# Four images through a windowed-attention layer: side work handed out by counts and due dates

## The chip, the core and the metric

The kernel runs on one core of one Trainium2 chip. The core has five engines that run their own instruction streams and meet at semaphores: TensorE (PE in the profile; its weight loads are PEld), VectorE (DVE), ScalarE (ACT), GpSimd (POOL) and SyncE (SP), which here issues the DMA transfers. The metric is the device time of one execution in microseconds (us); a kernel's time is the median of its runs.

## The reference, cut to what matters

The program is one forward pass over 4 images of 64 x 64 tokens with 128 channels, through four layers. The change lies in the last one, layer 3. What it computes, for each image (4096 tokens):

```python
t = t + L2_ffn(...)                      # the end of layer 2: its last addition is made in layer 3's loop
# attention over overlapping windows of 144 tokens, a new one each 72 tokens (55 windows)
xb  = ln(t) @ w_down.T + b_down          # 128 -> 16 channels
q, k, v = split(xb[windows] @ in_proj_w.T + in_proj_b)     # 4 heads of 4 channels
att = softmax(q k^T / 2) v, projected, the windows added back and divided by their overlap
out = ln(t) + sigmoid(gate) * (att @ w_up.T + b_up)
t   = t + ln(out) * gamma + beta
# a mixture of 8 experts, the best 2 of them for each token
p   = softmax(ln(t) @ router_w + router_b); top 2 of p, made to sum to 1
t   = t + sum over the two of p_e * (ln(t) @ expert_w[e] + expert_b[e])
```

Everything is float32. The work on one image does not depend on another image; only the steps inside one image follow each other.

## The kernel before

Layers 0 to 2 and the weights of layer 3 take the first 8.4 ms and are not touched. `layer3` then holds four images `b` = 0 to 3, each of which passes through these pieces:

- **Blocks** (first half of `front`, L2120 on): 8 blocks of 512 tokens. For each: `combined` (4 matmuls, L2038, and an addition on DVE), `statistics` (DVE, and a power on POOL, L2007), `normalise` (4 ACT instructions, L2017), four transposes (L2024), a copy on ACT (L2140), `downward` (4 matmuls, L2049). Each block needs about 7 `yield`s, 57 in all. The result `xb` (16 channels) goes to DRAM (`xb_d`).
- **Parts** (the rest of `front`): `windows` reads `xb_d` back, laid over partitions (8 DMAs, L2063); 16 empty steps; `queries`, 5 groups of 12 steps, makes `kt`, `qm`, `vt` with matmuls (L2179, L2185, L2195) and ACT copies (L2165).
- **Local attention**: 14 window groups for an image, four quarters each. `largest` (L2224) makes scores for their maxima (DVE, L2230), `weights` (L2266) makes scores and ACT's exponentials (L2273), `values` (L2291) multiplies with v, `divided` (L2311) divides.
- **Back** (`back`, L2351 on): 16 steps of transposes (L2358), then 8 blocks of 5 steps with matmuls (L2376), the layer norm, and the addition to `t`.
- **Chosen** (`chosen`, which calls `some` twice, once for each half image, L2407 on): the experts. A half begins with about 34 steps of layer norm, router matmuls (L2429) and the choice of two experts, then come 4 blocks with 4 transposes and 4 bias matmuls (L2480, L2489) and 8 expert matmuls of 128 x 512 (L2500), each followed by four DVE instructions that add the weighted result to the token tile `tex` (L2506). Images 0 to 2 do this with `own_bank`, one PSUM bank under the name `x`; image 3 does it in `last`, with `free_bank`, two PSUM buffers under the name `s`.

These pieces are Python generators. The order on TensorE is the order in which the code emits (the loop stands under `manual_schedule` for PE); the order on the other engines is found by the scheduler of the language from what PE's order and the data ask for.

**The loop.** `T` runs over 56 window groups (14 for each image), with `largest` four groups ahead, and `x` over 4 quarters. In this text X = 4(T + 4) + x numbers the quarters: 0 to 247, and 56 X are one image's share of `largest`. Beside the attention instructions each X holds five calls of `step(light)` and four calls of `step(heavy)`; a call takes the first generator of the list one `yield` further. `light` holds the fronts and backs, `heavy` the experts. With 57 + 76 steps a front takes some 27 X; after it `light` is empty until the image's attention has ended (`merged`, at X = 76, 132, 188 and 244), where `passed(b - 1)`, which is `back` and, behind its last step, the hand-over of `chosen` to `heavy`, and then the front of image b + 1 are put into `light` together. A front that isn't done when its image's `largest` begins (X = 56, 112, 168) is run to its end there. After the loop the rest of both lists is emitted in turns.

Of the kernel before, what the change touches and what calls it, by code (L numbers as in the profile page):

```python
# [14 lines left out]
P = 128  # L15
B = 4
HW = 64
S = HW * HW
NT = S // P
D = 128  # L20
# [28 lines left out]
DK = 16  # L49
# [11 lines left out]
def tl(pool, shape, tag, dtype=F32, bufs=None):  # L61
    return pool.tile(shape, dtype, name=tag, tag=tag, bufs=bufs)
# [1780 lines left out]
NM = (NW + G3 - 1) // G3  # L1843
# [102 lines left out]
def layer3(cm, kit, xa, wt_d, oe_d, x2, out):  # L1946
# [6 lines left out]
    with ExitStack() as ctx:  # L1953
        ctx.enter_context(nc.allow_non_contiguous_dma(reason="windows laid over partitions"))
        bp = ctx.enter_context(tc.tile_pool(name="cb", bufs=1))
# [8 lines left out]
        dr = ctx.enter_context(tc.tile_pool(name="cdram", bufs=2, space=DRAM))  # L1964
# [3 lines left out]
        wq4, wk4, f, mroot = [kit[n] for n in ("wq4", "wk4", "f", "mroot")]  # L1968
# [20 lines left out]
        def rows(a, b, k):  # L1989
            return a[b, k * BLK : (k + 1) * BLK, :].rearrange("(t p) c -> p t c", p=P)  # L1990

        def block(a, b, k, tag="tin"):
            t = tl(tp, [P, 4, D], tag)
            nc.sync.dma_start(t, rows(a, b, k))
            return t

        def statistics(src, who=""):

            st = tl(p2, [P, 4, 6], "ln_st" + who)
            mv = tl(p2, [P, 4, 2], "ln_mv" + who)  # L2000
            rs = tl(p2, [P, 2, 4], "ln_rs" + who)
            for i in range(4):
                nc.vector.bn_stats(st[:, i, :], src[:, i, :])
            for i in range(4):
                nc.vector.bn_aggr(mv[:, i, :], st[:, i, :])
            nc.vector.tensor_scalar(rs[:, 0, :], mv[:, :, 1], 1e-5, None, ALU.add)  # L2006
            nc.gpsimd.tensor_tensor(  # L2007
                rs[:, 0, :], rs[:, 0, :], mroot.to_broadcast([P, 4]), ALU.pow
            )
            nc.vector.scalar_tensor_tensor(  # L2010
                rs[:, 1, :], mv[:, :, 0], -1.0, rs[:, 0, :], ALU.mult, ALU.mult
            )
            return rs

        def normalise(dst, src, rs):
            for i in range(4):
                nc.scalar.activation(  # L2017
                    dst[:, i, :], src[:, i, :], AF.Identity,
                    bias=rs[:, 1, i : i + 1], scale=rs[:, 0, i : i + 1],
                )  # L2020

        def turned4(ps, src):
            for i in range(4):
                nc.tensor.transpose(ps[:, i * P : (i + 1) * P], src[:, i, :], cm.ident)  # L2024

        img = {}

        def gates(b, k):
            half = slice((b % 2) * E2, (b % 2 + 1) * E2)
            w = tl(tp, [P, BLK], "w")  # L2030
            nc.sync.dma_start(w[half, :], wt_d[half, b // 2, k * BLK : (k + 1) * BLK])
            return w

        def combined(b, k, t, w, ps):

            half = slice((b % 2) * E2, (b % 2 + 1) * E2)
            for i in range(4):
                nc.tensor.matmul(  # L2038
                    ps[:, i * P : (i + 1) * P], lhsT=w[half, i * P : (i + 1) * P],
                    rhs=oute[half, b // 2, :], start=True, stop=True,  # L2040
                )
            flat = t.rearrange("p i c -> p (i c)")
            nc.vector.tensor_tensor(flat, flat, ps, ALU.add)
            nc.sync.dma_start(rows(x2, b, k), t)
# [13 lines left out]
        def windows(xb_d, i):  # L2058
            for par in range(2):
                nw = (min(NM, NW - i * NM) + 1 - par) // 2  # L2060
                t0 = (i * NM + par) * STRIDE
                m0 = par * NM // 2
                nc.sync.dma_start(  # L2063
                    f[32 * i : 32 * i + DK, m0 : m0 + nw, :].rearrange(
                        "c m (j d) -> c (m j) d", d=DK
                    ),
                    xb_d[t0 : t0 + nw * WIN, :].rearrange("(m c) d -> c m d", c=DK),
                )

        def fresh(b):  # L2070
            img[b] = {"xl": tl(dr, [1, S, D], "xl_d"), "t": tl(dr, [1, S, D], "t_d")}
            return img[b], tl(bp, [P, NT, DK], "xb"), tl(dr, [S, DK], "xb_d")

        def first(b):

# [44 lines left out]
        def front(b, bank):  # L2120

            me, xb, xb_d = fresh(b)
            t, w = block(xa, b, 0), gates(b, 0)
            yield
            for k in range(NBLK):
                combined(b, k, t, w, bank())
                yield
                if k + 1 < NBLK:
                    nt, nw = block(xa, b, k + 1), gates(b, k + 1)
                rs = statistics(t)  # L2130
                yield
                yield
                xl = tl(tp, [P, 4, D], "xl")
                normalise(xl, t, rs)
                nc.sync.dma_start(rows(me["xl"], 0, k), xl)
                yield
                ps = bank()
                turned4(ps, xl)
                xT = tl(p2, [P, BLK], "xT")
                nc.scalar.copy(xT, ps)  # L2140
                yield
                yield
                downward(bank(), xT, xb, k)
                t, w = nt, nw
                yield
            nc.sync.dma_start(xb_d.rearrange("(t p) d -> p t d", p=P), xb)

            for i in range(G):
                windows(xb_d, i)
            for _ in range(16):
                yield
            yield from queries(b, bank, (nc.scalar.copy,))
# [244 lines left out]
        def chosen(b, bank):  # L2401

            me = img[b]
            for half in range(2):
                yield from some(me["t"], b, NB * half, bank)
# [110 lines left out]
        AHEAD = 4  # L2516
        LAST = B * NM
        light, heavy = [], []

        def step(todo):  # L2520
            while todo:
                try:
                    next(todo[0])
                    return
                except StopIteration:
                    todo.pop(0)

        def passed(b, bank):

            yield from back(b, bank)  # L2530
            if b + 1 < B:
                heavy.append(chosen(b, own_bank))

        def last():

            for half in range(2):
                while img[B - 1].get("done", 0) < NB * (half + 1):
                    yield
                yield from some(img[B - 1]["t"], B - 1, NB * half, free_bank)


        with tc.manual_schedule(engines={mybir.EngineType.PE}):
            first(0)
            fronts = {1: front(1, shared_bank)}
            light.append(fronts[1])
            for T in range(-AHEAD, LAST + 2):
                b, m = divmod(T + AHEAD, NM)
                if m == 0 and 0 < b < B:
                    while fronts[b] in light:
                        step(light)  # L2550
                for x in range(4):
                    if 0 < T <= LAST:
                        values(T - 1, x)
                    step(heavy)
                    step(light)
                    if x % 2 == 0 and T + AHEAD < LAST:
                        largest(T + AHEAD, x // 2)
                    step(light)
                    if x == 2 and T % 2 == 0 and 1 < T + AHEAD <= LAST:
                        turned(T + AHEAD - 1)  # L2560
                    step(heavy)
                    step(light)
                    if x == 2 and 0 < T <= LAST:
                        divided(T - 1, 0)
                    if x == 0 and 1 < T:
                        divided(T - 2, 1)
                        b, m = divmod(T - 1, NM)
                        if m == 0:
                            merged(b - 1)
                            light.append(passed(b - 1, shared_bank))  # L2570
                            if b + 1 < B:
                                fronts[b + 1] = front(b + 1, shared_bank)
                                light.append(fronts[b + 1])
                    step(heavy)
                    step(light)
                    if 0 <= T < LAST:
                        weights(T, x // 2, x % 2)
                    step(heavy)
                    step(light)
            heavy.append(last())  # L2580
            while light or heavy:
                step(light)
                step(heavy)


# [98 lines left out]
```

## Time and profile before

| | us |
|---|---|
| median of 3 runs (10190.57 to 10219.28) | 10200.37 |
| the profiled execution | 10193.03 |
| its span, first to last instruction | 10191.1 |
| layer 3's loop and tail within the span | 8424.6 to 10191.1 |

The whole program keeps PE busy for 85% of the span, DVE for 74%, ACT for 52% and POOL for 53%; the mean granted TensorE clock is 0.907 of full speed. Layer 3 is the last 1766 us, 17% of the span, and there PE is busy most.

The stages of layer 3 can be found in the trace by the `weights` matmuls of L2266: 1792 are recorded, eight for each of the 224 X from 16 to 239. The first group starts at 8539.2 us (X = 16), and counting on gives each X a time: X = 26 at 8590.6, 56 at 8684.4, 76 at 8750.6, 88 at 8826.4, 112 at 9035.3, 132 at 9148.0, 144 at 9251.9, 168 at 9451.4, 188 at 9574.0, 200 at 9675.2 and 239 at 9872.6.

### The profile page before, as it was taken

Reading aid. Unit: us, or ns where it says so; the run is one execution under the profiler, and the core shown is the slowest. Engines: PE = TensorE matmul, PEld = TensorE weight load, DVE = VectorE, ACT = ScalarE, POOL = GpSimd, SP = SyncE. Lnnn points to the kernel's source line nnn. Section 1 sums busy time; section 2 is a strip of 40 time slices with the busy share of each in tenths; the row PEclk is TensorE's granted clock in tenths of the full one; section 3 lists DMA queues with packets and bytes.
Section 4 is the critical chain, followed back from the end, with each engine's and each line's share of the span. In section 5 each row is a group of like instructions: output and inputs, shape, how many; then the busy total and the mean of one; then the engine's idle time right before and its main releaser. Section 6 shows DMA issues by size and latency. Waiting matters only on the chain.

```text
span 10191.1 us, 193260 instructions
## 1 busy us (share of the span) xinstructions
PE 8632.5 (85%) x73048; PEld 4244.2 (42%) x73048; DVE 7500.6 (74%) x11046; ACT 5339.3 (52%) x13284; POOL 5376.2 (53%) x2789
## 2 busy tenths in 40 slices
PE   7888988889988898888788659999999857888876
PEld 3333444444434444444333434444444434544442
DVE  4999999999999999999999666354541123455556
ACT  5775545665556665466422237676776513433331
POOL 4999999899999899998999300000000000100000
PEclk8999999999999999999998779999999977797887
DMA  7344543445543455444323311111100161213101
GB/s 209 104 133 128 141 132 115 124 132 144 151 115 122 122 155 146 127 121 119 95 88 93 113 52 36 37 36 37 32 24 27 45 202 36 56 27 69 42 24 47
DMA packets 1081627, 957.38 MB, mean 94 GB/s; under 512 B 165356, under 2 KB 825616, under 8 KB 1073920
## 3 DMA queue, kind: packets, MB, share of 16 engines
q1 hardware_dynamic: 1055298, 880.82, 29.3%
q0 software_dynamic: 18560, 63.37, 3.3%
q8 instruction: 586, 9.60, 0.4%
q14 instruction: 337, 2.76, 0.1%
q10 hardware_dynamic: 6846, 0.83, 0.1%
HBM read 608.77 MB, written 335.80 MB: 93 GB/s over the span
## 4 chain that ended last, share of the span: by engine, by line
PE 42%; DVE 27%; POOL 9%; issue 8%; ACT 6%; DMA 5%; SPq 2%; DVEq 0%; ACTq 0%; POOLq 0%
DVE big L869 15%; POOL big L884 8%; PE qk L1653 7%; PE av L1712 7%; PE yp L904 5%; PE db L849 5%; DVE tex L2506 2%; PE x L2500 2%; PE s L2266 2%; DVE du L825 2%; DVE mx L2230 1%; PE po L2291 1%; PE bg L383 1%; DMA xo<-xT_d 1%; DVE db L864 1%
## 5 line engine op out<-in xcount | busy, mean ns | idle before, releaser
L884 POOL TENSOR_TENSOR big<-big,ct 128x2048 f32<-128x2048 f32 x1024 | 4659.3, 4550 | 76.2 <-PE db L849 0.2
L869 DVE TENSOR_TENSOR_SCAN big<-dA,db 128x1024 f32<-128x1024 f32 x2048 | 4570.9, 2273 | 11.8 <-DMA xo<-xT_d 8.8
L849 PE MATMUL db<-dg,du 32*64 32x256 f32 x32768 | 1908.6, 417 | 639.9 <-DVE big L869 500.4
L904 PE MATMUL yp<-big,both 128*64 128x256 f32 x16384 | 2206.8, 416 | 63.1 <-ACT yc L918 50.9
L904 PEld LDWEIGHTS yp<-big,both 128*64 128x64 f32 x16384 | 1184.9, 148 | 1022.5 <-issue 547.7
L849 PEld LDWEIGHTS db<-dg,du 32*64 32x64 f32 x32768 | 655.4, 134 | 1838.3 <-issue 1737.2
L1712 PE MATMUL av<-e,x 128*128 128x512 f32 x2048 | 974.0, 592 | 4.6 <-ACT e L1707 4.6
L1653 PE MATMUL qk<-a,xT 128*128 128x512 f32 x2048 | 966.6, 594 | 8.6 <-ACT e L1657 7.9
L1657 ACT ACTIVATE e<-qk,nk 128x512 f32<-128x512 f32 x1024 | 692.8, 685 | 533.8 <-PE qk L1653 532.7
L918 ACT COPY yr<-yp 128x64 f32<-128x64 f32 x1024 | 221.4, 216 | 1417.7 <-PE yp L904 1402.0
L817 ACT ACTIVATE dg<-mask,BT 128x32 f32<-128x32 f32 x4096 | 896.6, 318 | 11.0 <-PE db L849 8.8
L772 ACT ACTIVATE dA<-dp,A 128x252 f32<-128x252 f32 x2048 | 866.1, 498 | 62.2 <-issue 42.6
L1232 POOL TENSOR_TENSOR g_rs<-g_rs,qrow 128x4 f32<-128x4 f32 x32 | 41.1, 1283 | 1500.0 <-DVE g_rs L1231 1500.0
L1653 PEld LDWEIGHTS qk<-a,xT 128*128 128x128 f32 x2048 | 378.0, 190 | 462.3 <-issue 357.7
L1712 PEld LDWEIGHTS av<-e,x 128*128 128x128 f32 x2048 | 381.6, 190 | 434.8 <-issue 393.7
L1707 ACT ACTIVATE e<-e 128x1024 f32<-128x1024 f32 x510 | 538.7, 1056 | 15.4
L876 POOL TENSOR_TENSOR cy<-big,a 128x32 f32<-128x32 f32 x1008 | 364.1, 361 | 317.5 <-DVE big L869 265.1
L2273 ACT ACTIVATE e<-s 128x576 f32<-128x576 f32 x448 | 275.5, 648 | 472.6 <-PE s L2266 470.9
L2285 POOL COPY vp<-vt 112x80 f32<-112x80 f32 x112 | 30.8, 275 | 848.0 <-PE po L2291 821.9
L2007 POOL TENSOR_TENSOR ln_rs<-ln_rs,mroot 128x4 f32<-128x4 f32 x64 | 65.3, 1021 | 743.8 <-DVE ln_rs L2006 526.4
L2506 DVE SCALAR_TENSOR_TENSOR tex<-x,gw,tex 128x128 f32<-128x128 f32 x768 | 264.2, 344 | 236.2 <-PE x L2500 221.0
L825 DVE TENSOR_TENSOR du<-xo,dt 128x256 f32<-128x256 f32 x512 | 385.9, 754 | 0.0
(563 smaller groups left out, 9907.2 us busy)
## 6 DMA issues: line engine op xcount, KB each, us to landing
ct<-ct_d SPq DMA_DIRECT2D x1024, 128.0 KB
xo<-xT_d SPq DMA_DIRECT2D x2048, 32.0 KB
dg_d<-dg SPq DMA_DIRECT2D x256, 256.0 KB
dg<-dg_d SPq DMA_DIRECT2D x256, 256.0 KB
t4k<-xc_d SPq DMA_DIRECT2D x288, 132.0 KB
dp<-dl_d SPq DMA_DIRECT2D x256, 128.0 KB
dT_d<-t2k SPq DMA_DIRECT2D x256, 128.0 KB
dt<-dT_d SPq DMA_DIRECT2D x512, 64.0 KB
```

Of the source, the lines that this page charges most:

```text
L772: nc.scalar.activation(w["dA"][:, :, g, n, 1:], w["dp"][:, g, :, 1:], AF.Exp, scale=A[:, w["h"], g, n : n + 1],)
L817: nc.scalar.activation(q["dg"][:, n, :], mask, AF.Copy, scale=BT[:, q["c"], n : n + 1])
L825: nc.vector.tensor_tensor(q["du"], q["xo"], q["dt"].unsqueeze(1).to_broadcast([P, 2, P]), ALU.mult)
L849: nc.tensor.matmul(bs[j][p * TC : (p + 1) * TC, g * NH0 : (g + 1) * NH0, t0 : t0 + QR], lhsT=q["du"][rows, kp, g * TC : (g + 1) * TC], rhs ...
L869: nc.vector.tensor_tensor_scan(st[:, u].rearrange("p n t -> p (n t)"), q["w"]["dA"][:, c % QC].rearrange("p g n t -> p (g n t)"), bs[j].re ...
L884: nc.gpsimd.tensor_tensor(sv, sv, q["ct"].rearrange("p n t -> p (n t)").unsqueeze(1) .to_broadcast([P, 4, NH0 * TC]), ALU.mult,)
L904: nc.tensor.matmul(yp[p * TC : (p + 1) * TC], lhsT=both, rhs=st[:, :, p * NH0 + n, :], start=(n == 0), stop=(n == NH0 - 1),)
L1653: nc.tensor.matmul(ps, lhsT=me["xT"][:, kt * P : (kt + 1) * P], rhs=me["a"][k], start=True, stop=True,)
L1657: nc.scalar.activation(e[:, j, :], ps, AF.Exp, bias=me["nk"][:, kt : kt + 1], scale=2.0)
L1707: nc.scalar.activation(es[g + 2], es[g + 2], AF.Exp)
L1712: nc.tensor.matmul(avs[b, k], lhsT=img[b]["x"][:, kt, :], rhs=e[:, j, :], start=(kt == 0), stop=(kt == NT - 1),)
L2506: nc.vector.scalar_tensor_tensor(t[:, i, :], s[:, e * D : (e + 1) * D], gw[:, j, 4 * a + e : 4 * a + e + 1], t[:, i, :], ALU.mult, ALU.add,)
```

## The change

The change touches only the order in which layer 3's generators are advanced.

- `front` is cut in two. `front` keeps the blocks and the store of `xb`; the new generator `parts` holds `windows`, the 16 empty steps and `queries`. The DRAM buffers `xl`, `t` and `xb_d` are now separate for each image (they shared two).
- Entries of `light` carry a name, a count of steps left and a due X. `wanted` goes through the list and, for each entry, divides the steps left up to and with it by the X left until its due date, rounded up; the largest is the quota of this X. `lights()` is called at the same five places as `step(light)` was, and advances by `lit()` so that the quota is spread over the five.
- The blocks of image b + 1 are queued when image b's `largest` begins (X = 56 and 112), due 20 X later; its parts, at the end of image b - 1's attention (X = 76, 132) behind the back, due at X = 112 and 168. A back is due 11 X after it was queued. For image 1, blocks are due at X = 28 and parts at X = 56.
- `heavy` is advanced as before. `passed` still hands `chosen` over behind its last counted step.

```diff
+        def parts(b, bank):
 
             for i in range(G):
-                windows(xb_d, i)
+                windows(img[b]["xb_d"], i)
             for _ in range(16):
                 yield
             yield from queries(b, bank, (nc.scalar.copy,))
...
+        def queue(name, gen, left, due):
+            light.append({"name": name, "gen": gen, "left": left, "due": due})
+
+        def lit():
+            while light:
+                e = light[0]
+                try:
+                    next(e["gen"])
+                    e["left"] = max(0, e["left"] - 1)
+                    return
+                except StopIteration:
+                    light.pop(0)
+
+        def wanted(X):
+            sum, most = 0, 0
+            for e in light:
+                sum += e["left"]
+                most = max(most, -(-sum // max(1, e["due"] - X)))
+            return most
+
         def passed(b, bank):
 
             yield from back(b, bank)
             if b + 1 < B:
                 heavy.append(chosen(b, own_bank))
...
+        BLOCKS, PARTS, BACK, SLOTS = 57, 76, 56, 5
+        turn = 4 * NM
 
         with tc.manual_schedule(engines={mybir.EngineType.PE}):
             first(0)
-            fronts = {1: front(1, shared_bank)}
-            light.append(fronts[1])
+            queue(1, front(1, shared_bank), BLOCKS, turn // 2)
+            queue(1, parts(1, shared_bank), PARTS, turn)
             for T in range(-AHEAD, LAST + 2):
                 b, m = divmod(T + AHEAD, NM)
                 if m == 0 and 0 < b < B:
-                    while fronts[b] in light:
-                        step(light)
+                    while any(e["name"] == b and e["due"] <= b * turn for e in light):
+                        lit()
+                    if b + 1 < B:
+                        queue(b + 1, front(b + 1, shared_bank), BLOCKS, b * turn + 4 * AHEAD + 4)
                 for x in range(4):
+                    X = 4 * (T + AHEAD) + x
+                    quota, done = wanted(X), [0, 0]
+
+                    def lights():
+                        done[0] += 1
+                        while done[1] < done[0] * quota // SLOTS:
+                            lit()
+                            done[1] += 1
+
                     if 0 < T <= LAST:
                         values(T - 1, x)
                     step(heavy)
-                    step(light)
+                    lights()
...
                         if m == 0:
                             merged(b - 1)
-                            light.append(passed(b - 1, shared_bank))
+                            queue(-1, passed(b - 1, shared_bank), BACK, X + BACK // SLOTS)
                             if b + 1 < B:
-                                fronts[b + 1] = front(b + 1, shared_bank)
-                                light.append(fronts[b + 1])
+                                queue(
+                                    b + 1, parts(b + 1, shared_bank), PARTS, (b + 1) * turn
+                                )
...
             heavy.append(last())
             while light or heavy:
-                step(light)
+                lit()
                 step(heavy)
```

More of the change, by code (lines that the diff above doesn't have):

```diff
@@ L2070, in fresh @@
         def fresh(b):
-            img[b] = {"xl": tl(dr, [1, S, D], "xl_d"), "t": tl(dr, [1, S, D], "t_d")}
-            return img[b], tl(bp, [P, NT, DK], "xb"), tl(dr, [S, DK], "xb_d")
+            img[b] = {
+                "xl": tl(dr, [1, S, D], f"xl_d{b}", bufs=1),
+                "t": tl(dr, [1, S, D], f"t_d{b}", bufs=1),
+                "xb_d": tl(dr, [S, DK], f"xb_d{b}", bufs=1),
+            }
+            return img[b], tl(bp, [P, NT, DK], "xb"), img[b]["xb_d"]
         def first(b):
@@ L2554, in layer3 @@
                     step(heavy)
-                    step(light)
+                    lights()
                     if x % 2 == 0 and T + AHEAD < LAST:
                         largest(T + AHEAD, x // 2)
-                    step(light)
+                    lights()
                     if x == 2 and T % 2 == 0 and 1 < T + AHEAD <= LAST:
@@ L2561, in layer3 @@
                     step(heavy)
-                    step(light)
+                    lights()
                     if x == 2 and 0 < T <= LAST:
@@ L2569, in layer3 @@
                             merged(b - 1)
-                            light.append(passed(b - 1, shared_bank))
+                            queue(-1, passed(b - 1, shared_bank), BACK, X + BACK // SLOTS)
                             if b + 1 < B:
-                                fronts[b + 1] = front(b + 1, shared_bank)
-                                light.append(fronts[b + 1])
+                                queue(
+                                    b + 1, parts(b + 1, shared_bank), PARTS, (b + 1) * turn
+                                )
                     step(heavy)
-                    step(light)
+                    lights()
                     if 0 <= T < LAST:
@@ L2578, in layer3 @@
                     step(heavy)
-                    step(light)
+                    lights()
             heavy.append(last())
             while light or heavy:
-                step(light)
+                lit()
                 step(heavy)
```

## The prediction

> **What bounds the kernel now.** I read the page first, then the busy times in windows cut at the X of layer 3, then the timeline of TensorE at the places where the windows differ. In the page's 40 slices layer 3 is the last seven; TensorE is the busiest engine there, but neither full nor at full clock.
>
> ```profile
> span 10191.1 us, 193260 instructions
> ...
> PE   7888988889988898888788659999999857888876
> ...
> PEclk8999999999999999999998779999999977797887
> ```
>
> The windows (length, busy us of PE, PEld, DVE, ACT and POOL, granted clock, DMA) are X 0-15, 16-25, 26-74, 76-87, 88-98, 102-111, 114-131, then X 200 to the first transpose of image 3's back, from there to the end of image 2's experts, and image 3's experts:
>
> ```profile
> 8424.60:8539.20 114.60, 67.60 (x403) 50.23 (x401) 38.04 (x117) 20.89 (x46) 8.06 (x8) 0.54 0.42 76
> 8539.20:8590.60 51.40, 50.22 (x411) 23.15 (x410) 11.33 (x17) 26.08 (x49) 0.53 (x2) 1.00 0.01 2
> 8590.60:8743.30 152.70, 138.10 (x1855) 83.02 (x1854) 61.06 (x115) 69.30 (x122) 6.36 (x24) 1.00 0.01 3
> 8750.60:8826.40 75.80, 57.87 (x579) 37.92 (x578) 45.99 (x162) 35.92 (x76) 13.62 (x17) 0.75 0.28 80
> 8826.40:8933.10 106.70, 89.33 (x630) 62.46 (x630) 47.58 (x219) 41.55 (x88) 10.67 (x15) 0.62 0.33 90
> 8954.70:9035.30 80.60, 78.64 (x542) 35.78 (x541) 36.81 (x96) 31.03 (x60) 2.60 (x7) 1.00 0.05 14
> 9048.40:9148.00 99.60, 80.51 (x796) 43.72 (x795) 56.31 (x207) 33.53 (x64) 4.69 (x12) 0.90 0.07 21
> ...
> 9675.20:9901.90 226.70, 180.84 (x1617) 93.75 (x1618) 116.88 (x459) 75.56 (x146) 10.88 (x25) 0.88 0.08 23
> 9901.90:10014.00 112.10, 70.76 (x194) 37.21 (x194) 63.51 (x225) 20.85 (x49) 10.07 (x10) 0.56 0.22 61
> 10014.00:10191.10 177.10, 110.06 (x321) 50.82 (x319) 112.93 (x462) 21.13 (x46) 6.04 (x6) 0.82 0.12 35
> ```
>
> To be seen: attention alone costs 152.7 / 49 = 3.12 us per X, TensorE 90% busy; with image 0's experts beside it 99.6 / 18 = 5.54; with queries too 80.6 / 10 = 8.06. Where blocks or a back run beside it, the clock falls to 0.54-0.75: TensorE waits, and then runs at half speed. The timeline shows the waits that matter below: one for the windows' transfer, expert steps in the one bank `x` at full clock (two rows) and at half clock (two rows), and in the two buffers `s` (two rows).
>
> ```profile
> 8529.25 1.78 PE L2179 MATMUL mm<-f,wk 128*128 128x432 f32 x2 [12.33 <-DMA f<-xb_d]
> ...
> 9881.35 1.10 PE L2500 MATMUL x<-ew,x3T 128*128 128x512 f32 x2 [1.07 <-DVE tex L2506]
> 9884.14 1.10 PE L2500 MATMUL x<-ew,x3T 128*128 128x512 f32 x2 [1.69 <-DVE tex L2506]
> ...
> 10008.42 2.04 PE L2500 MATMUL x<-ew,x3T 128*128 128x512 f32 x2 [1.89 <-DVE tex L2506]
> 10012.16 2.04 PE L2500 MATMUL x<-ew,x3T 128*128 128x512 f32 x2 [1.70 <-DVE tex L2506]
> ...
> 10049.33 2.13 PE L2500 MATMUL s<-ew,x3T 128*128 128x512 f32 x4 [0.80 <-DVE tex L2506]
> 10052.25 2.13 PE L2500 MATMUL s<-ew,x3T 128*128 128x512 f32 x4 [0.79 <-DVE tex L2506]
> ```
>
> A step in `x` is 2.79 us at full clock (9884.14 - 9881.35) and 3.74 at half; in `s` it is 2.92 / 2 = 1.46.
>
> **The change, part by part.** No instruction is added; all is order. The decisive part is one that the text does not announce. Image 2's back is queued at X = 188 with 56 steps and due 11 X later, and nothing stands behind it in `light` (no fourth front). When its 56 counted steps are used, `left` is 0, the quota is 0, and `lit` isn't called; but the hand-over of `chosen(2)` lies behind the 56th step, in a 57th call. That call comes only when image 3's back is queued at X = 244. The order of the built program says the same: between X = 202 and 239 TensorE has attention alone, and all 128 expert steps of images 2 and 3 stand behind the last window. For images 0 and 1 `parts` stands behind the back and calls it on, so their experts start in time.
>
> *1. What leaves X 200 on.* Now 226.7 us. Left are: X 200 and 201 with image 1's last experts, 2 x 5.54 = 11; 22 X at 3.12 = 69; 16 X without `largest`, of which no row is free of experts: TensorE's instructions alone are 0.77 + 0.70 + 0.30 = 1.77 us, and X with few expert steps took 2.31 to 2.41, so 2.0 x 16 = 32 (28 to 38); the last five X with values alone, 8 (five times 0.70 to 2.4: 4 to 12). Together 120, a saving of 107 (97 to 115).
>
> *2. What comes behind the last window.* Image 2's experts, all of them, with image 3's back beside the first part. Back and router phase with the first 3 expert steps: the back cost 75.8 - 12 x 3.12 = 38 us beside attention, and 98 (9901.9 to 10000) beside expert steps now; I take 65, as its DVE work and the router's must both pass. Then 29 steps in `x` and 3 changes of block, then the second half: router phase 28.7 (10099.3 to 10128.0, image 3), 32 steps and 4 changes. A change adds 5.1 (8.82 from 9929.61 to 9938.43, less 3.74). At half clock: 65 + 29 x 3.74 + 15 + 28.7 + 32 x 3.74 + 20 = 357. At full clock, changes at 4: 65 + 93 + 29 + 105 = 292. Now these pieces take 112.1, so +245 (+180). I take half clock, since the nearest row, where `x` steps stand without attention, has it all through:
>
> ```profile
> 9968.40:10014.00 45.60, 26.43 (x55) 12.75 (x56) 26.15 (x100) 8.70 (x21) 5.74 (x6) 0.50 0.23 64
> ```
>
> TensorE never waited over 3.1 us in that stretch. The Trainium skill (TensorE: Matmul & The Clock Gate, "HAM oscillation — how this bites in real kernels") blames idle gaps of more than about 3.4 us for the half clock; by that rule the lone steps, with gaps of 1.7, would keep full speed, and the end would come 65 us earlier. The row speaks against it here.
>
> Image 3's own experts stay at 177. The tail is longer by 245 - 107 = 138 (73 at full clock).
>
> *3. The levelled stages up to X = 200*, each against its window now:
> - Image 1, X 0-55, now 259.8. A block is a chain of 10.7 us (8 from 8425.6 to 8511.2); 7 of them are now spread over X 0-15: 77 with the start. Then 40 X of attention 125, one block 8 (2.8 to 10.7), queries 27 (51.4 - 31.2 = 20 for 50 of 60 steps, and waits). 237: gain 23 (10 to 35). The 12.33 of waiting for the windows is in it: 16 empty steps at 2 to 3 per X now pass beside attention.
> - Image 2's blocks at X 56-75, beside attention alone: TensorE's work is 8 x 2.8 = 22 at full clock; beside experts the blocks cost 106.7 - 11 x 5.54 = 46 now. 35 (22 to 46) is lost here; ACT, DVE (28 of 66 us busy) and POOL have room.
> - X 88-111, now 208.9: experts 24 x 5.54 = 133 and queries at half their pace, 22 (15 to 30; 25 for 50 steps now): gain 54 (46 to 61).
> - Image 3's blocks at X 112-131: cost beside experts 40 (35 to 46).
> - X 144-167, now 199.5: 133 + 22: gain 44 (37 to 50). X 168-187, now 122.6: without the front's run to its end, 20 x 5.54: gain 11 (0 to 14).
> - Three backs at 6 steps per X instead of 5: a shorter stage, but its chain through DVE, POOL and ACT stays; gain 9 (-15 to 24).
> - SP: the eight window loads of images 2 and 3 now stand behind a back's loads and stores instead of behind the store of `xb`, and token loads stand behind them; eight took 8.03 us to issue. Covered by some 4 X without a query; 0, at worst 8 for each. Separate DRAM buffers: no wait for one shows among TensorE's waits; 0.
>
> Gain: 23 - 35 + 54 - 40 + 44 + 11 + 9 = 66 (-14 to 127, SP's 16 apart).
>
> *Sum:* 138 - 66 = +72, on the profiled execution's 10193: 10265. That execution stands 7 us (0.07%) below the median, less than the sum can resolve.
>
> **The rivals.**
> - *A. The tail keeps full clock.* Then +73 - 66 = +7: 10200, no change. For it: 9876 to 9897, when values still stood between the steps, was at full clock. Against: the row at 0.50.
> - *B. Levelling gains nothing:* blocks and queries cost the same TensorE time wherever they stand, and stalls move with them. +138: 10331. For it: PE is in order, and blocks beside experts return in X 112-131. Against: queries at 1.00 clock show PE work fills well.
> - *C. Faster: the clock stays at full speed through all of layer 3,* because a spread load never lets TensorE rest long enough. Then three backs win the PE time lost to half clock (57.9 x 0.25 + 85.4 x 0.21 + 80.9 x 0.19 = 47), blocks cost 22 each instead of 35 and 40 (31), and the tail is +73: 73 - 66 - 78 = -71: 10122. It decides for faster once levelling gains over 104 with the tail at full clock. For it: 1.00 at X 26-74. Against: the backs wait for DVE and ACT with nothing else beside them, at 0.75.
> - *D. The late hand-over doesn't happen:* -66, 10127. The built order excludes it.
>
> **How the numbers follow.** Forecast case (+30 to +110) 0.52, A 0.19, B and worse 0.20, C 0.09. 0.3%, about what a measurement of this kernel tells from no change, is 31 us: slower 0.72, same 0.19, faster 0.09. The range reaches from A's 10200 to B's 10331 and leaves out C with the lower half of A, and what lies above B.
>
> **What will show it.** No L2500 between X = 202 and the last window, whose X take 3.1 and then 2.0 us; 128 such steps behind it; the `x` steps among them 3.74 us apart at clock 0.5; more than 480 us from the first back transpose of image 3 to the end (now 289). X = 200 some 66 us earlier. X 88-111 near 155 us, X 56-75 near 100. It is wrong if the steps stand 2.8 apart, or if X = 200 comes over 110 us earlier or no earlier than now.

## The result, and the profile after

| | before | changed |
|---|---|---|
| median of 6 runs, us | 10203.02 | 10234.82 |
| from, to | 10190.57, 10219.28 | 10229.04, 10250.16 |
| ratio, with its 95% interval | | 1.0032 (1.002 to 1.0045) |
| profiled execution; span | 10193.03; 10191.1 | 10231.87; 10230.0 |

The changed kernel is slower by 0.3%, 32 us. The forecast was slower, 10265. The page after (span, busy tenths of TensorE, granted clock) has its last two slices at 5 and 6 tenths busy and at 0.5 and 0.7 of the clock; before they were at 7 and 6, and at 0.8 and 0.7:

```profile
span 10230.0 us, 193304 instructions
...
PE   7888998889988899888887559999999768888856
...
PEclk8899999999999999989899779999999877789857
```

The windows after, cut at the same X (length, busy us of PE, PEld, DVE, ACT, POOL, clock, DMA): X 0-15, 16-25, 26-55, 56-75, 76-87, 88-111, 112-131, 132-143, 144-167, 168-187, 188-199.

```profile
8417.50:8495.40 77.90, 52.80 (x360) 41.95 (x359) 33.96 (x102) 17.37 (x37) 7.05 (x7) 0.54 0.29 83
8495.40:8538.00 42.60, 39.10 (x349) 23.98 (x348) 14.23 (x31) 16.18 (x29) 1.54 (x3) 0.64 0.47 42
8538.00:8656.90 118.90, 115.26 (x1259) 60.82 (x1257) 37.24 (x64) 55.24 (x104) 4.26 (x16) 1.00 0.01 3
8656.90:8771.50 114.60, 104.95 (x916) 69.39 (x915) 45.22 (x151) 45.21 (x90) 10.67 (x18) 0.64 0.27 73
8771.50:8850.80 79.30, 62.91 (x581) 41.55 (x581) 48.76 (x170) 38.34 (x82) 13.38 (x17) 0.70 0.45 85
8850.80:8998.10 147.30, 137.41 (x1176) 71.07 (x1176) 76.68 (x249) 57.25 (x110) 5.20 (x14) 0.95 0.08 23
8998.10:9128.70 130.60, 110.01 (x1026) 68.00 (x1025) 78.44 (x320) 53.22 (x109) 13.70 (x21) 0.86 0.27 74
9128.70:9233.50 104.80, 77.63 (x640) 43.23 (x639) 73.76 (x244) 37.59 (x79) 11.67 (x16) 0.82 0.37 85
9233.50:9370.00 136.50, 130.49 (x1165) 67.67 (x1165) 73.02 (x239) 57.22 (x111) 5.15 (x14) 1.00 0.07 20
9370.00:9482.00 112.00, 89.86 (x876) 50.18 (x875) 63.47 (x235) 38.03 (x73) 6.69 (x14) 0.88 0.08 23
9482.00:9585.00 103.00, 77.41 (x642) 43.28 (x641) 73.86 (x244) 37.22 (x79) 11.66 (x16) 0.82 0.27 75
```

The same windows before that the prediction does not show whole, X 56-75, 88-111, 112-131 and 144-167:

```profile
8684.40:8750.60 66.20, 57.88 (x774) 35.03 (x774) 28.43 (x58) 28.45 (x50) 2.65 (x10) 0.99 0.01 3
8826.40:9035.30 208.90, 187.30 (x1319) 108.48 (x1319) 95.14 (x340) 77.76 (x157) 13.27 (x22) 0.78 0.29 57
9035.30:9148.00 112.70, 89.90 (x881) 47.90 (x880) 65.08 (x237) 36.39 (x69) 5.70 (x13) 0.91 0.07 21
9251.90:9451.40 199.50, 180.76 (x1310) 102.54 (x1309) 91.82 (x330) 74.44 (x151) 12.25 (x21) 0.82 0.26 53
```

X = 200 now comes at 9585.0 instead of 9675.2: 90 us early. The rest, in a second set of windows: image 2's experts with image 3's back; image 3's experts; and from X = 200 to the first transpose of image 3's back.

```profile
9698.20:10051.20 353.00, 198.00 (x439) 87.91 (x440) 145.56 (x574) 40.69 (x93) 15.95 (x15) 0.51 0.11 31
10051.20:10230.00 178.80, 111.45 (x321) 51.13 (x319) 113.00 (x462) 21.15 (x46) 6.04 (x6) 0.81 0.12 34
...
9585.00:9698.20 113.20, 101.87 (x1369) 59.13 (x1369) 39.80 (x104) 56.58 (x102) 5.78 (x19) 1.00 0.03 8
```

These 645.0 us were 515.9. The tail takes back the 90 and 39 more. TensorE's timeline in the middle of the 353 us shows why:

```profile
9807.88 2.05 PE L2502 MATMUL x<-ew,x3T 128*128 128x512 f32 x2 [1.69 <-DVE tex L2508]
9811.62 2.04 PE L2502 MATMUL x<-ew,x3T 128*128 128x512 f32 x2 [1.70 <-DVE tex L2508]
9815.36 2.04 PE L2502 MATMUL x<-ew,x3T 128*128 128x512 f32 x2 [1.70 <-DVE tex L2508]
```

One step each 3.74 us: 2.05 of matmul at half clock, 1.70 of waiting for the four DVE instructions that empty the one bank `x`, and nothing else to emit.

### The profile page after: what moved, and what is told of

The parts are those of the page before. It is cut to its first block, busy times and chain, and to the rows that moved or that the text cites. A ratio compares the mean times of both kernels' runs of the same rounds, so it can differ in the third digit from the quotient of the medians.

```text
span 10230.0 us, 193304 instructions
## 1 busy us (share of the span) xinstructions
PE 8627.8 (84%) x73048; PEld 4232.2 (41%) x73048; DVE 7505.8 (73%) x11046; ACT 5341.0 (52%) x13284; POOL 5375.3 (53%) x2789
## 5 line engine op out<-in xcount | busy, mean ns | idle before, releaser
L2502 PE MATMUL x<-ew,x3T 128*128 128x512 f32 x384 | 288.3, 842 | 175.3 <-DVE tex L2508 160.3
```

Source lines behind the costliest of these rows:

```text
L2502: nc.tensor.matmul(s, lhsT=x3T[:, j * P : (j + 1) * P], rhs=ew[:, 4 * a : 4 * a + 4, :].rearrange("p e c -> p (e c)"), start=True, stop=True,)
```

## The experiments

Theory at the start: two effects of opposite sign that add, the late hand-over of image 2's experts (+129 us by the traces) and the levelling up to X = 200 (-90, 7 of which lie ahead of layer 3's first scores, in code that is not touched). Rivals: that one is no effect of its own. Times are compared with runs of the kernel before on the same chip. The first four kernels:

**E1, the hand-over in time.** From the changed kernel:

```diff
-        BLOCKS, PARTS, BACK, SLOTS = 57, 76, 56, 5
+        BLOCKS, PARTS, BACK, SLOTS = 57, 76, 57, 5
```

> The changed kernel with a back counted as 57 steps instead of 56, so that the call that hands an image's experts over is among the counted ones; image 2's experts then start near X = 200, as in the kernel before. Theory (the levelled stages gain, and the late hand-over of image 2's experts costs 129 us of it): X = 200 at about 9585, as in the changed kernel, and the rest as long as in the kernel before (516 us): 10110, within 10095 to 10130. Rival (the 90 us that the levelled stages are early are no gain of their own and are given back once experts run beside the last image's attention): about 10200.

10168.22, ratio 0.9964 (0.9953 to 0.9976). It lies between the two: faster than before, but only 33 us of the expected 90. The windows tell where most of the rest went, and it is not the tail (524.7 us from X = 200 on, 515.9 before): X 88-111 takes 167.4 us (changed kernel 147.3), X 112-131 151.4 (130.6), X 144-167 162.7 (136.5). The last, E1's:

```profile
9275.00:9437.70 162.70, 145.57 (x1167) 74.77 (x1167) 75.35 (x250) 59.38 (x114) 6.27 (x15) 0.92 0.06 18
```

Against the changed kernel's row it has 11 us more of idle TensorE and 15 us more of busy at a lower clock, with the same instructions. The difference lies in the order on TensorE. One call earlier for the hand-over also moves every expert step by one of the four heavy slots of an X. Written as letters (E expert step, V values, L largest, q query, D divided, | weights), two X of each:

```
changed kernel   E V L q E D | E q V E q
E1               V E L q D E | q V E E q
```

Up to the last window, 29 expert steps in E1's order follow another with nothing between them, in the changed kernel none, in the kernel before 23. E1's timeline has such a pair, the second step after 1.70 us of waiting; in the changed kernel's timeline, in the same X, steps stand apart and queries or values pass in between:

```profile
9382.44 0.70 PE L2293 MATMUL po<-e,vp 128*32 128x144 f32 x16
9383.07 1.13 PE L2502 MATMUL x<-ew,x3T 128*128 128x512 f32 x2
9385.89 1.10 PE L2502 MATMUL x<-ew,x3T 128*128 128x512 f32 x2 [1.70 <-DVE tex L2508]
9386.83 1.62 PE L2187 MATMUL mm<-f,wq 128*128 128x432 f32 x2
```
```profile
9323.15 1.10 PE L2502 MATMUL x<-ew,x3T 128*128 128x512 f32 x2 [0.70 <-DVE rec L2331]
9324.09 1.62 PE L2187 MATMUL mm<-f,wq 128*128 128x432 f32 x2
9325.63 0.70 PE L2293 MATMUL po<-e,vp 128*32 128x144 f32 x16
9326.26 1.13 PE L2502 MATMUL x<-ew,x3T 128*128 128x512 f32 x2
```

A third effect, then: the phase of the expert steps. E5, E6 and E9 below test it.

**E2, the late hand-over alone.** From the kernel before:

```diff
         def passed(b, bank):
 
+            if b == B - 1:
+                heavy.append(chosen(b - 1, own_bank))
             yield from back(b, bank)
-            if b + 1 < B:
+            if b + 2 < B:
                 heavy.append(chosen(b, own_bank))
```

> The kernel before with one thing of the changed one: image 2's experts are handed over only when image 3's back is queued at X = 244. Theory: the cost of the late hand-over does not depend on the levelling: 129 us more than the kernel before, 10332, within 10315 to 10350, with expert steps 3.74 us apart in the tail. Rival (the two parts of the change act on each other, and alone the late hand-over costs no more than the whole change): about 10235.

10336.81, ratio 1.014 (1.0117 to 1.0163): 135 us slower, as the theory had it; X = 200 stands at 9671.9 (before 9675.2), and TensorE's steps in the tail look like the changed kernel's:

```profile
9901.49 2.04 PE L2500 MATMUL x<-ew,x3T 128*128 128x512 f32 x2 [1.69 <-DVE tex L2506]
9905.23 2.05 PE L2500 MATMUL x<-ew,x3T 128*128 128x512 f32 x2 [1.69 <-DVE tex L2506]
```

The late hand-over costs the same without the levelling.

**E3, two buffers in the tail.** From the changed kernel, the hand-over still late:

```diff
-                heavy.append(chosen(b, own_bank))
+                heavy.append(chosen(b, own_bank if b + 2 < B else free_bank))
```

> The changed kernel, but image 2's experts, late as they are, use the two buffers s instead of the one bank x. Theory (the tail is long because a step waits for the four DVE instructions of the step before, in one bank, at half clock): 64 steps of 3.74 fall to 1.46 (full clock) or 1.9 (half), less what back takes beside the first ones: 110 to 140 us less, 10095 to 10125. Rival (the tail is long because nothing covers it, whatever the bank): less than 40 us gained, 10195 or more.

10094.94, ratio 0.9896 (0.9877 to 0.9915): 138 us less than the changed kernel (each against the kernel before), and faster than before. Pairs of steps are now 2.92 us apart, 1.46 for each, at full clock:

```profile
9817.14 2.13 PE L2502 MATMUL s<-ew,x3T 128*128 128x512 f32 x4 [0.80 <-DVE tex L2508]
9820.06 2.13 PE L2502 MATMUL s<-ew,x3T 128*128 128x512 f32 x4 [0.80 <-DVE tex L2508]
```

So being late is not costly by itself; being late in one bank with nothing beside it is.

**E4, the clock of the tail.** From the changed kernel, `over` being set behind the last window:

```diff
                         s = bank()
                         nc.tensor.matmul(s, ...)
+                        if bank is own_bank and over:
+                            for _ in range(2):
+                                nc.tensor.matmul(
+                                    po.rearrange("p j q -> p (j q)"), lhsT=cm.ident,
+                                    rhs=ew[:, 0:3, :].rearrange("p e c -> p (e c)")[:, 0 : 2 * WIN],
+                                    start=True, stop=True,
+                                )
```

> The changed kernel with two matmuls of 128 x 288 without a reader behind each of image 2's expert matmuls in the tail, so that TensorE rests less between the steps. Theory (the half clock in the tail follows from TensorE's rests, and costs 0.95 us a step): the granted clock of that stretch rises to 1.0, steps are 2.8 apart: 50 to 65 us less, 10170 to 10185. Rival (the clock is not set by these rests): clock stays 0.5, the fillers take 2.4 us where 1.7 were idle, steps 4.4 apart: some 40 us more, 10275.

10178.49, ratio 0.9981 (0.9972 to 0.9991): 55 us less than the changed kernel. Work without use makes the kernel faster, because the clock opens: the stretch of these steps (9751 to 9985) has 0.88, and steps stand 2.79 apart.

```profile
9802.15 1.10 PE L2502 MATMUL x<-ew,x3T 128*128 128x512 f32 x2 [0.72 <-DVE tex L2515]
9803.08 1.13 PE L2509 MATMUL po<-ew,ident 128*128 128x288 f32 x4
9804.94 1.10 PE L2502 MATMUL x<-ew,x3T 128*128 128x512 f32 x2 [0.72 <-DVE tex L2515]
```

Next, the phase. The same edit, one empty step ahead of image 0's experts, goes into three kernels, so that phase and levelling are each seen with and without the other:

```diff
             me = img[b]
+            if b == 0:
+                yield
             for half in range(2):
                 yield from some(me["t"], b, NB * half, bank)
```

**E5, the hand-over in time, and the other phase** (E1 with this edit):

> The kernel with the hand-over in time, and one empty step ahead of image 0's experts, so that every expert step stands one heavy slot later: as in the changed kernel an expert step never follows another without attention work between them on TensorE, while in the first version 29 pairs were adjacent. Theory (the 55 us missing from the first version were lost because a step in the one bank waits 1.7 us for DVE, and what stands between two steps hides it): windows X 88 to 111, 112 to 131 and 144 to 167 return to 147, 131 and 136 us, from 167, 151 and 163: 10100, within 10085 to 10120. Rival (the loss came from something else that the earlier hand-over brings): 10150 or more.

10091.44, ratio 0.9888 (0.9872 to 0.9905): the windows are 149.9, 136.9 and 141.7 us, from 167.4, 151.4 and 162.7 in E1. The first returned to what the changed kernel had; the other two came within 5 to 6 us of it. It is 1.1% ahead of the kernel before; with E3 (0.9896), from which its interval does not tell it apart, it is the fastest of the study. X 144-167 in E5:

```profile
9230.40:9372.10 141.70, 136.14 (x1167) 70.81 (x1167) 73.13 (x239) 57.17 (x111) 5.14 (x14) 0.95 0.07 21
```

**E9, the changed kernel in the old phase** (the changed kernel with this edit):

> The changed kernel with one empty step ahead of image 0's experts: they go back to the phase of the kernel before, 22 adjacent pairs, everything else as changed. Theory (part of what the change gained up to X = 200 is the phase that its counts happened to give): 55 to 70 us slower than the changed kernel, 10295, in the windows X 88 to 132 and 144 to 167. Rival (the gain is the levelling's own): within 15 us of 10235.

10276.01, ratio 1.0072 (1.0055 to 1.0089): 44 us slower than the changed kernel (each against the kernel before), less than the 55 expected and far from the rival's 15. It is in X 88-111 (168.1 us, from 147.3) and 144-167 (154.3, from 136.5):

```profile
8854.10:9022.20 168.10, 151.74 (x1177) 77.15 (x1177) 76.72 (x247) 58.26 (x112) 5.20 (x14) 0.90 0.07 20
9022.20:9155.80 133.60, 113.37 (x1028) 69.42 (x1027) 78.08 (x323) 52.88 (x109) 13.74 (x21) 0.85 0.28 75
...
9259.50:9413.80 154.30, 139.66 (x1165) 70.12 (x1166) 73.74 (x239) 57.81 (x111) 5.18 (x14) 0.96 0.07 20
```

X 112-131, the middle row, hardly moved (133.6, from 130.6), though in E1, in the same phase, it took 151.4 at a clock of 0.73. What sets that window is not settled by the phase alone.

**E6, the kernel before in the other phase** (the kernel before with this edit):

> The kernel before with the same one empty step ahead of image 0's experts: 23 adjacent pairs become none, and nothing else of the change is in it. Theory (gaps): beside queries at five light steps per X little waits are left to hide, and where experts stand beside attention alone the sum of waits is the same in both phases (2.7 us per two X), so 10 to 25 us less: 10185. Rival (the phase is worth the same whatever stands beside): 50 to 70 us less, 10140.

10191.18, ratio 0.9989 (0.998 to 0.9999): 9 us less, at the edge of what can be measured. With five light steps in each X the old order had other work between nearly all pairs where queries stand: only 1 of its 23 adjacent steps lies in X 88-111 or 144-167, where E1 has 9 and E9 has 12. So the phase was worth little there. Phase and spreading act together: three light steps per X leave pairs bare that five covered.

**E7, two buffers for what remains behind the last window** (E5, with the bank changed to `s` once the last window is emitted):

```diff
+        def either_bank():
+            return free_bank() if over else own_bank()
...
-                heavy.append(chosen(b, own_bank))
+                heavy.append(chosen(b, either_bank))
```

> The kernel with the hand-over in time and the other phase, whose image 2 changes from the one bank x to the two buffers s once the last window is emitted, when s is free. Theory (a step falls from 3.74 to 1.5 to 1.9 us behind the last window): 16 to 20 steps remain there, 30 to 45 us less than without it: 10065. Rival (image 3's back beside them is what takes the time there): less than 15 us.

10100.48, ratio 0.9893 (0.9876 to 0.9909): no gain over E5. In the profiles the part from X = 239 on is 18 us shorter (294.2 against 312.3), between the rival's 15 and the theory's 30. But parts whose code is the same took longer by more than that: layer 3 starts 12 us later (8434.8 against 8422.9), and X 56-75 and 76-87 take 6 and 9 us more, at clocks of 0.64 and 0.70 (0.70 and 0.83 in E5). Inconclusive; the gain is as small as what such parts vary from run to run.

**E8, the blocks not early** (E5, with the blocks queued behind the back again):

```diff
-                    if b + 1 < B:
-                        queue(b + 1, front(b + 1, shared_bank), BLOCKS, b * turn + 4 * AHEAD + 4)
...
                             if b + 1 < B:
+                                queue(
+                                    b + 1, front(b + 1, shared_bank), BLOCKS, (b + 1) * turn
+                                )
                                 queue(
                                     b + 1, parts(b + 1, shared_bank), PARTS, (b + 1) * turn
                                 )
```

> The kernel with the hand-over in time and the other phase, without the early blocks: the blocks of images 2 and 3 are queued again behind the back of the image before the last (X = 76, 132), and share the 36 X to their due date with it and the parts. Against the same kernel with early blocks (10091): X 56 to 75 is 43 us shorter and X 112 to 131 some 26, and X 88 to 111 and 144 to 167 are longer by 45 each, what blocks cost there in the kernel before. Theory (a block costs much the same wherever it stands, so the early start is worth little of the whole): 0 to 40 us slower, 10110. Rival (the early start is the larger part of the gain up to X = 200): 50 us slower or more, 10145.

10147.63, ratio 0.9952 (0.9935 to 0.9968): against the kernel before, 47 us less where E5 has 109 less. The early start of the blocks is worth about 62 us, as the rival had it; my estimate of 0 to 40 was too low. Its windows X 56-75, 76-87, 88-111, 112-131 and 144-167:

```profile
8659.80:8722.70 62.90, 56.96 (x764) 34.33 (x764) 26.10 (x53) 28.43 (x50) 2.64 (x10) 1.00 0.01 3
8722.70:8812.70 90.00, 64.05 (x621) 44.26 (x621) 54.02 (x194) 42.45 (x92) 15.59 (x19) 0.72 0.33 93
8812.70:9011.70 199.00, 181.31 (x1288) 105.14 (x1287) 93.07 (x332) 70.55 (x140) 12.18 (x21) 0.78 0.27 50
9011.70:9115.60 103.90, 86.61 (x876) 47.57 (x875) 60.48 (x216) 36.13 (x69) 4.67 (x12) 0.90 0.07 20
9225.80:9422.70 196.90, 176.84 (x1297) 103.25 (x1296) 88.77 (x325) 71.86 (x145) 12.30 (x21) 0.81 0.28 50
```

Blocks and queries together beside experts take the clock down to 0.78 and 0.81, where queries without blocks had 0.93 and 0.95 in E5; X 88-111 and 144-167 grow by 49 and 55, and the early places shrink by 46 and 33. That makes some 25 of the 53 us between the two profiles; another 19 are X 76-87, where image 2's blocks now share the time with the back (90.0 against 70.7, though this window took up to 79.6 in other runs), and 8 are X 132-143, the same place of image 3 (110.2 against 101.8).

**E10, denser blocks** (E5, with one matmul without a reader in each of image 2's blocks):

```diff
                 combined(b, k, t, w, bank())
+                if b == 2:
+                    nc.tensor.matmul(
+                        own_bank(), lhsT=cm.ident,
+                        rhs=ew[:, 0:4, :].rearrange("p e c -> p (e c)"),
+                        start=True, stop=True,
+                    )
```

> The kernel with the hand-over in time and the other phase, and in each of image 2's blocks one matmul of 128 x 512 without a reader behind the four of combined. X 56 to 75 has a granted clock of 0.64 to 0.71 in the runs so far although TensorE is busy for 90% of it. Theory (the clock there depends on how much of the array's time such matmuls fill, and a dense one opens it again): clock 0.9 or more, the window 100 us or less instead of 109. Rival (the clock is not moved by it): clock below 0.75, the window 8 x 1.1 to 2.05 longer, 118 to 125.

10104.82, ratio 0.9913 (0.9897 to 0.993). In X 56-75 the clock is 0.82, up from 0.70 in E5, but the window takes 113.5 us, not less than E5's 108.6:

```profile
8652.60:8766.10 113.50, 97.31 (x932) 60.13 (x931) 44.13 (x148) 44.86 (x90) 10.75 (x18) 0.82 0.26 73
```

Neither expectation holds: the clock moved as the theory said, less than half way, and the window did not get shorter. Where the blocks are early and have no added matmul, the same window took 105.6 to 114.7 us at clocks of 0.64 to 0.77 in the other profiles, so that one profile shows a small rise of the clock and nothing about the time.

## Why the prediction was right

The direction and the mechanism held. Against the terms of the sum, on the profiled executions (10231.87 - 10193.03 = +39, where +72 was summed):

| term | predicted | measured |
|---|---|---|
| X = 200 to image 3's back | 120 us long | 113.2 |
| image 2's experts with that back | 357 | 353.0 |
| image 3's experts | 177 | 178.8 |
| the tail in all | +138 | +129 |
| image 1, X 0-55 | -23 | -20 |
| image 2's blocks, X 56-75 | +35 | +48 |
| X 88-111 | -54 | -62 |
| image 3's blocks, X 112-131 | +40 | +18 |
| X 144-167 | -44 | -63 |
| X 168-187 | -11 | -11 |
| three backs | -9 | +6 |
| start of layer 3 | 0 | -7 |
| X = 200 in all | -66 | -90 |

- *The total.* The misses partly cancel: terms that came out dearer than summed (image 2's blocks and the backs above all) add some 31 us, those that came out cheaper, and the earlier start, take off some 65. That the total is not further off than 33 us is in that measure luck; the direction is not, since the tail was the largest term. The start of layer 3 belongs to no term: it lies behind code that is the same, and from 8415.6 to 8437.2 us in the profiles of all these kernels. So some 83 of the 90 us are the levelling's.
- *The uncounted 57th call* is shown: E1 mends the count and nothing else, and image 2's experts stand beside the last image's attention again; E2 puts the lateness alone into the kernel before and costs 135 us. The two measurements of the same thing, E2 against before (+135) and the changed kernel against E5 (+32 + 109 = +141), agree, so lateness and levelling add.
- *The price of a lone step, 3.74 us at half clock*, was the term that decided between slower and no change, and it came out to the hundredth. The parts of the 357 came out too: 67 us to the fourth step (65 in the sum), 27 for the second router phase (28.7). The rule on idle gaps of the Trainium skill (TensorE: Matmul & The Clock Gate, "HAM oscillation — how this bites in real kernels"), weighed in the prediction, would have made it 2.79; the measurement decides against it here. The stretch behind image 3's back had clock 0.50 for 285.7 us, with gaps of 1.7 us between most matmuls (second row; the first is taken up in the last section). Two gaps in it are over 3.4 us, 3.54 and 7.48 in the second router phase, but they come late: the clock had been full for 3.4 us (third row), fell at 9758.2 beside waits of 1.65 and 2.38, and was at 0.50 for 137.6 us before the first of the two (fourth row).

```profile
8713.00:8747.30 34.30, 32.71 (x262) 21.40 (x260) 9.98 (x34) 12.53 (x25) 3.03 (x6) 0.50 0.23 66
9765.50:10051.20 285.70, 158.67 (x254) 55.71 (x255) 105.52 (x385) 16.37 (x36) 7.05 (x7) 0.50 0.06 19
9754.80:9758.20 3.40, 1.24 (x3) 0.30 (x2) 2.85 (x13) 0.00 (x0) 0.52 (x1) 1.00 0.51 146
9758.20:9895.80 137.60, 78.29 (x128) 28.39 (x128) 52.54 (x164) 9.38 (x21) 3.51 (x4) 0.50 0.08 23
```

  That the clock is what made 2.79 into 3.74 is shown by E4.
- *The step that was mis-sized* is the third, "the levelled stages": three of its terms lie outside their own bounds, by 17 us (X 112-131), 13 (X 144-167) and 2 (X 56-75), and X 88-111 by less than 1. I priced queries and blocks beside experts with what they cost in the kernel before, as if it were a property of the work. It depends on the order on TensorE: an expert step in one bank leaves 1.7 us that other work can fill, and the changed kernel's counts happened to give a phase in which almost every gap is filled. E9 takes that phase away: X 144-167 rises to 154.3 us, near the 155 of the prediction, and X 88-111 past it, to 168.1. For X 112-131 the phase is not the explanation, since E9 leaves it at 133.6; it stays open.
- *Blocks beside attention alone* were dearer than taken, 48 us (39 to 48 in the profiles of the kernels with early blocks, E10 aside), near the upper bound: the window ran at a clock of 0.64 to 0.77, while I hoped for part of the full clock.
- *The backs* were not shorter with six steps per X. The first of them took 79.3 us here, 75.8 before, and 70.7 to 79.6 in the other kernels whose blocks are early, so the +6 is no more than they vary. That their chain through DVE, POOL and ACT sets the pace, as the lower bound had it, is argued and not tested alone.
- *The terms at nothing* held as far as the trace shows: up to X = 200 TensorE waits for no DMA in the changed kernel, and the 12.33 us for the windows are gone. The separate DRAM buffers were not run without the rest of the change.
- *Rivals.* A (full clock in the tail) falls by the 0.50. B (levelling gains nothing) falls by X = 200, 90 us early, and by E5, which keeps 109 us of gain once the hand-over is mended. C needed the full clock in the tail and more than 104 us of levelling; the levelling gave some 83, and the clock was not there. D is E1's or E5's kernel, not this one.

## What to carry to other kernels

A quota that counts `yield`s must count the call behind the last `yield` too, where a generator hands work on; whether it did is seen in the built order of one engine, without a time. A short wait inside each step costs next to nothing beside a stream that fills it (X 144-167: 6 us of idle TensorE in 24 X) and its full length where the step stands alone (1.70 us of 3.74), so look at what is left over at the end of a program and give it the buffers that are free by then (E3: 138 us by one line). And when steps of two streams are interleaved by slots, one slot of phase can be worth more than the whole change (76 us between E1 and E5).

## What the runs showed of the hardware that I had not expected

- TensorE ran faster with useless work: the lone steps kept it busy for 55% of the time, with a wait of 1.7 us in each, at clock 0.50; two matmuls without a reader in each step cut the wait to 0.72 us, and the clock of the stretch rose to 0.88 and the step fell to 2.79 (E4).
- Half clock also holds where TensorE hardly rests. In X 56-75 of the changed kernel the trace has a stretch of 34 us at 0.50 with TensorE busy for 32.7 of them and no wait over 1.2 us, the first of the four rows above (8713.0 to 8747.3). As the clock fell, it had just waited 2.33 us for DVE; attention alone, which also rests 10% of its time, but never over 1.0 us at once, stayed at 1.00 for 150 us in the kernel before. What brings the clock back is not the busy share of the trace alone; which property of the matmuls it is, E10 did not settle.
